# First layer of a graph network on one core: waits taken apart in a loop of two interleaved streams, long rows stored, edge weights and two-pass operations spread out

## The chip, the cores and the metric

The kernel runs on one core of one Trainium2 chip. The metric is the device time of one execution in microseconds; the figure for a kernel is the median of its timed runs. The engines go by the names of the profile: PE is TensorE (PEld its weight loads), DVE is VectorE, ACT is ScalarE, POOL is GpSimd, SP is SyncE. Each engine runs its own instructions in order and waits on semaphores for the others; a DMA is issued from one engine's queue (SP, ACT or POOL).

## The reference

A graph of 3125 nodes (256 features) and 100,000 edges, sorted by destination, goes through four blocks, each with a residual: a graph attention block, a mixture of experts of which two are shared by all tokens, a block of graph convolutions, and a mixture of experts routed by token. Only the first attention layer of the first block is touched here:

```python
h = (x @ W).reshape(N, H, C)                  # H = 4 heads of C = 256
al_s = jnp.einsum('nhc,hc->nh', h, a_src)
al_d = jnp.einsum('nhc,hc->nh', h, a_dst)
e = jax.nn.leaky_relu(al_s[src] + al_d[dst], NEG_SLOPE)
m = jax.ops.segment_max(e, dst, num_segments=N)
ex = jnp.exp(e - m[dst])
denom = jax.ops.segment_sum(ex, dst, num_segments=N)
alpha = ex / denom[dst]
out = jax.ops.segment_sum(h[src] * alpha[:, :, None], dst, num_segments=N)
```

The edges include one loop for each node. Here `x` is the layer-normed input and `W` is 256 by 1024.

## The kernel before

`FirstLayer.run` does the first attention layer. It sums normed input rows by edge and multiplies by `W` afterwards, so an edge costs a row of 256 numbers and four weights, not 1024 numbers. The edges come in 391 chunks (`C1`) of 256, sorted by destination. Three streams of work are interleaved by hand in one loop:

- **Counting** (`count_step`, all 391 chunks). It makes a matrix of how often each pair of nodes is joined, which later layers use. `make` builds two one-hot matrices for a chunk: `hot_key` on DVE (L1668), and `hot_lo` either on DVE (L1671) or, for two chunks in three after the first 20, on ACT in two passes, Abs (L1674) and Relu (L1677). `multiply` takes their product on PE (L1685). The product's columns go into the accumulator `acc` at a place that is read from a register: `keep` copies all columns but the first on ACT (L1702), and `add` adds the first column on DVE (L1707), because the first column may already hold counts of the chunk before. In round i the chunk i is made, i - 1 multiplied, i - 3 added and i - 2 kept.
- **Edges** (`edge_step`, chunks from 108 on, 283 of them, in batches of four). `fetch` gathers table rows of the sources on POOL (L1794, two gathers a chunk) into a ring of 12 chunks; a gather is issued once PE has used the slot's old rows. `window` fetches the destination terms of a batch and the places of its edges (L1804, L1807, on SP's queue). `pick_terms` (PE, L1831) lays a term beside each edge; `weigh_edges` adds source terms (DVE, L1840), takes the two slopes' maximum (DVE, L1843) and the exponent (ACT, L1844); `spread_edges` (DVE, L1850) puts the weights into the matrix that `multiply_edges` (PE, L1864) multiplies by the rows; `add_edges` adds the result into `agg` (DVE, L1877). `place_edges` (L1815, L1818) prepares the places of the batch after the next.
- **Dense** (`dense_step`, 100 steps). The first 256 destinations have so many edges that their weights are made for all sources: `exponent` on ACT in two passes, slope (L2031) and exponent (L2033), `weigh` on DVE (L2038), and the product on PE (L2047).

A round of the loop is a count step, one small task (clearing a piece, or the product by `W`, L1990 with its copy L2001), as many edge steps as are due, and any dense steps that are due. `in_order` then fixes the order of PE, DVE and ACT as it was traced, so each engine's queue is the program's order; SP and POOL follow the scheduler. PSUM banks: three for counts, two for the edges' sums (`ps_edge`, a chunk takes bank c % 2), two for the dense sums (`ps_po1`), one for everything else (`ps_aux1`).

Ahead of the loop, under its own fixed order of DVE: the bounds of the chunks (`bounds`), the layer norm in five groups (`norm_rows`), `attention_vectors` (L1574: products of `W` by the attention rows, 16 for this layer and 16 for the next), `keys`, `edge_starts`, `check`, then PE transposes of the normed rows (L2147) and the products of them by the attention vectors (L2157). `first_terms` turns these into source terms (stored in 32-byte pieces beside the table's rows, L1602), destination terms (`terms`, L1606) and the loops' weights (`loops`, L1615); the last two are stored in pieces of 16 bytes, one for each node. `new_sums` starts each piece of `agg` from the loops (L1920 loads the weights, L1930 multiplies).

## Time and profile before

| | |
|---|---|
| median of 3 runs | 2530.73 us (2528.81 to 2531.22) |
| the profiled execution, its own time | 2545.83 us |
| its span, first to last instruction | 2544.0 us |
| mean granted TensorE clock | 0.91 |
| first layer, up to its last store | 0 to about 1072 us |
| its loop | about 105 to 1042 us |
| busy in the whole span | PE 2125.6, DVE 1361.0, ACT 1138.6, POOL 819.5 us |

A row of the profile names a line, an engine, an operation and its tiles; behind the bar stand its busy time and its mean duration, and behind the second bar the time for which the engine was idle just before it, with what ended that idle time. Line numbers are those of the kernel before; in the changed kernel the same operations stand 14 to 63 lines lower.

### The profile page before, as it was taken

The page shows a single profiled execution, that of the slowest core. Times are in us where ns is not written, and L with a number is a line of the kernel's source. Part 1 is how long each engine was busy: PE and PEld are TensorE (multiplying, and loading weights), DVE is VectorE, ACT ScalarE, POOL GpSimd, SP SyncE. Part 2 cuts the span into 40 slices and gives each one's busy share as a digit, 9 for nine tenths or more (in the row PEclk, how much of TensorE's full clock was granted, in tenths as well). Part 3 has the DMA queues.
Part 4 walks back from the last instruction along what each step waited for, and adds up shares of the span by engine and source line. Part 5 has one row for each costly group of instructions (what it writes and reads, how often), then busy time and mean ns, then how long its engine had stood idle before and what let it go on. Part 6 is the DMA issues. An engine that isn't in the chain of part 4 may idle for free. (4 is left out here: it accounts for less than half of the span.)

```text
span 2544.0 us, 36033 instructions
## 1 busy us (share of the span) xinstructions
PE 2125.6 (84%) x10501; PEld 1746.2 (69%) x10501; DVE 1361.0 (53%) x4372; ACT 1138.6 (45%) x2504; POOL 819.5 (32%) x803
## 2 busy tenths in 40 slices
PE   4377668777878778698999979998999897999996
PEld 3255556665656556487888858876887676888885
DVE  8767557556677667514888844343334665122221
ACT  3277545555555555352444425443434443222321
POOL 2655566656566766020000030000000313222221
PEclk8578888888998988899999989998999998899998
DMA  7633446464556656599222110003424436667773
GB/s 246 118 95 90 132 120 173 112 180 126 165 152 191 184 142 180 172 384 300 93 76 67 51 50 1 1 1 129 127 67 156 164 110 208 170 180 209 233 209 74
DMA packets 247282, 358.52 MB, mean 141 GB/s; under 512 B 47768, under 2 KB 188371, under 8 KB 243362
## 3 DMA queue, kind: packets, MB, share of 16 engines
q1 hardware_dynamic: 203906, 256.29, 31.9%
q0 software_dynamic: 39600, 95.33, 14.6%
q10 hardware_dynamic: 3568, 4.47, 0.7%
q8 instruction: 89, 1.46, 0.2%
q14 instruction: 119, 0.97, 0.1%
HBM read 270.26 MB, written 86.20 MB: 140 GB/s over the span
## 5 line engine op out<-in xcount | busy, mean ns | idle before, releaser
L1794 POOL DMA_INDIRECT edge_rows<-table,pick x566 | 594.1, 1050 | 329.2 <-issue 116.4
L1864 PE MATMUL edge_sums<-edge_moves,edge_rows 128*128 128x120 f32 x2264 | 362.3, 311 | 66.4 <-issue 33.8
L1864 PEld LDWEIGHTS edge_sums<-edge_moves,edge_rows 128*128 128x128 f32 x2264 | 335.8, 222 | 113.3 <-issue 50.3
L1092 PE MATMUL po<-parts,cnt_r 128*128 128x512 f32 x1250 | 318.3, 410 | 16.7 <-ACT cnt_r L1086 9.5
L1685 PE MATMUL ps<-hot_key,hot_lo 128*128 128x350 f16 (+2 forms) x782 | 210.4, 360 | 125.7 <-ACT hot_lo L1677 51.5
L1702 ACT CAST acc<-ps 128x325 f32 (+2 forms) x391 | 178.4, 456 | 262.4 <-DVE acc L1707 109.1
L1092 PEld LDWEIGHTS po<-parts,cnt_r 128*128 128x128 f32 x1250 | 240.1, 195 | 70.4 <-ACT cnt_r L1086 10.3
L854 PE MATMUL po<-h,w 128*128 128x257 f32 x1250 | 278.1, 383 | 7.2 <-DVE w L845 4.9
L854 PEld LDWEIGHTS po<-h,w 128*128 128x128 f32 x1250 | 236.8, 191 | 44.0 <-DVE w L845 6.9
L1668 DVE TENSOR_SCALAR hot_key<-iota_key,key 128x350 f16<-128x350 f16 (+2 forms) x782 | 233.0, 327 | 7.1 <-PE ps L1685 3.7
L2625 ACT ACTIVATE hid<-ph,ffn_b 128x256 f32<-128x256 f32 (+1 forms) x232 | 105.8, 456 | 263.5 <-PE ph L2623 257.9
L1685 PEld LDWEIGHTS <-hot_lo 128*128 128x128 f16 x782 | 76.0, 109 | 183.8 <-ACT hot_lo L1677 68.6
L2623 PE MATMUL ph<-xe,ffn_w 128*128 128x256 f32 (+1 forms) x928 | 194.4, 367 | 3.6 <-DMA ffn_w<-in_L_ffn_W 3.6
L2633 PE MATMUL py<-ffn_w,hid 128*128 128x256 f32 x848 | 189.8, 381 | 1.4 <-ACT hid L2625 1.4
L2638 POOL DMA_INDIRECT out<-y,to x53 | 82.6, 1559 | 316.8 <-DVE y L2637 162.4
L2623 PEld LDWEIGHTS ph<-xe,ffn_w 128*128 128x128 f32 x928 | 165.1, 194 | 26.9 <-DVE rt_xt L1023 4.0
L2633 PEld LDWEIGHTS py<-ffn_w,hid 128*128 128x128 f32 x848 | 159.3, 191 | 22.2 <-ACT hid L2625 1.8
L839 ACT ACTIVATE z<-z,att_cols 128x640 f32<-128x640 f32 x125 | 103.1, 828 | 153.5 <-DVE z L837 130.7
L1674 ACT ACTIVATE hot_lo<-iota_key,lo 128x128 f16<-128x128 f16 x494 | 169.0, 391 | 0.0
L1877 DVE TENSOR_TENSOR agg<-agg,edge_sums 128x126 f32 (+1 forms) x283 | 87.2, 308 | 133.0 <-PE ps L1685 35.3
L1086 ACT CAST cnt_r<-cnt_h 128x1920 fp32r<-128x1920 f16 x50 | 89.9, 1799 | 116.3 <-PE po L1092 106.0
L2299 POOL IOTA earlier<- 128x128 f32 x1 | 0.2, 243 | 395.7 <-PE po L1092 395.7
(410 smaller groups left out, 3295.1 us busy)
## 6 DMA issues: line engine op xcount, KB each, us to landing
ffn_w<-in_L_ffn_W SPq DMA_DIRECT2D x58, 1024.0 KB
cnt_h<-cnt SPq DMA_DIRECT2D x50, 800.0 KB
rows<-blank SPq DMA_DIRECT2D x109, 258.0 KB
cnt<-acc SPq DMA_DIRECT2D x50, 400.0 KB
cnt<-cnt SPq DMA_DIRECT2D x25, 800.0 KB
normed<-first_out SPq DMA_DIRECT2D x20, 640.0 KB
first_out<-first SPq DMA_DIRECT2D x56, 192.0 KB
edge_turn<-places SPq DMA_DIRECT2D x283, 32.0 KB
```

Of the source, the lines that this page charges most:

```text
L839: nc.scalar.activation(z, z, AF.Exp, bias=cols[:, 0, j:j + 1], scale=-1.0)
L854: nc.tensor.matmul(pos[i][:, :D + 1], lhsT=w[:, ts(i, P)], rhs=moving[:, j, :D + 1], start=(j == 0), stop=(j == NB - 1))
L1092: nc.tensor.matmul(pos[b], lhsT=c[:, j - j0, ts(b, P)], rhs=parts[i][:, j].rearrange("p a m -> p (a m)"), start=(j == 0), stop=(j == NB - 1))
L1668: nc.vector.tensor_scalar(h[:, u, :NB * w], self.wide[:, :NB * w], self.key[:, t:t + 1], None, op0=ALU.is_equal)
L1674: nc.scalar.activation(l[:, u, :], self.wide[:, :P], AF.Abs, bias=self.lo[:, t:t + 1], scale=-1.0)
L1685: self.nc.tensor.matmul(ps[:, :n], lhsT=l[:, u, :], rhs=h[:, u, :n], start=(u == 0), stop=(u == CT - 1))
L1702: self.nc.scalar.copy(self.acc[g][:, :, ds(o + 1, width(c) - 1)], self.parts[c][:, :, 1:])
L1794: self.nc.gpsimd.indirect_dma_start(out=self.ring[:, e % (RB * BT), :], out_offset=None, in_=self.table, in_offset=bass.IndirectOffsetOnAx ...
L1864: nc.tensor.matmul(ps[:, f * 4 * w:f * 4 * w + EW], lhsT=self.rows_of(m)[:, e, ts(f, P)], rhs=self.spread[m % 3][:, e * 5 * w:e * 5 * w + EW],
L2623: nc.tensor.matmul(ph, lhsT=w1[:, c, ts(f, P)], rhs=xe[:, c, :], start=(c == 0), stop=(c == 1))
L2625: nc.scalar.activation(hid[:, f, :], ph, AF.Gelu, bias=b1[:, f:f + 1])
L2633: nc.tensor.matmul(py, lhsT=hid[:, f, ts(i, P)], rhs=w2[:, f, :], start=(f == 0), stop=(f == NF - 1))
```

## The change

It has these parts, all in the first layer:

- `keep` and `add` are declared free of each other in one direction: the copy of a chunk no longer waits for additions of earlier chunks.
- The Relu of `hot_lo` moves into `sharpen`, behind `multiply`, `add` and `keep` of the round; the slope of a dense step is taken behind `make`, its exponent behind `sharpen`.
- The weights of a batch of edges: sum at the start of step 1, slopes' maximum at the end of step 1, exponent in step 2, spreading in step 3 of the batch before; it was sum, maximum and exponent at the end of step 0, spreading in step 2.
- The edges' sums go round four half banks; the dense sums have one bank and the rest two.
- The places of a batch come with one DMA instead of four. Registers are loaded four chunks ahead of their first use.
- At most one dense step is done in a round.
- Ahead of the loop: the attention vectors come before the norm, the rows are transposed and multiplied group by group right behind their norm, and the subtraction of the last row of `W` goes from POOL to DVE. The terms and the loops' weights are transposed on PE and stored as long rows.

```diff
     def where(self, name, c, row, n, engines, top):
 
         regs = self.regs
-        if (name, c) not in regs:
-            c8 = c // RG * RG
+        for c8 in (c // RG * RG, (c + RG // 2) // RG * RG):
+            if (name, c8) in regs or c8 >= n:
+                continue
             _, v = self.nc.values_load_multi_w_load_instructions(
...
+    def turn_rows(self, g, u1, pl, pool, turn):
+
+        nc, k = self.nc, self.k
+        xt = pool.tile([P, 2, GW], F32, name="xt", bufs=2)
+        for i in range(GB):
+            b, at = g * GB + i, ts(i, P)
+            pt = turn.tile([P, 512], F32, name="turn")
+            for c in range(2):
+                nc.tensor.transpose(pt[:, ts(c, P)], k.x[:, b, ts(c, P)], k.ident)
+            nc.scalar.copy(xt[:, :, at], pt[:, :2 * P].rearrange("p (c n) -> p c n", c=2))
+            for c in range(2):
+                nc.tensor.matmul(pl[:, 8 * b:8 * b + 8], lhsT=xt[:, c, at], rhs=u1[:, c, :],
+                                 start=(c == 0), stop=(c == 1))
+        nc.sync.dma_start(self.turned[:, :, g * GW:(g + 1) * GW], xt)
...
-        nc.sync.dma_start(self.terms.rearrange("o (b p k) -> (o p) b k", p=P, k=n), t)
+        pt = turn.tile([P, 512], F32, name="turn")
+        for i in range(n):
+            nc.tensor.transpose(pt[:NB, ts(i, P)], t[:, :, i], k.ident)
+        flat = tmp.tile([NB, P, n], F32, name="terms_flat")
+        nc.scalar.copy(flat, pt[:NB, :].rearrange("b (k p) -> b p k", k=n))
+        nc.sync.dma_start(self.terms.rearrange("o (b f) -> (o b) f", b=NB),
+                          flat.rearrange("b p k -> b (p k)"))
...
-        nc.sync.dma_start(self.loops.rearrange("(b p) k -> p b k", p=P), own)
+        pt = turn.tile([P, 512], F32, name="turn")
+        rows = (NB - DB) * n
+        nc.tensor.transpose(pt[:rows, :P], own.rearrange("p b k -> p (b k)"), k.ident)
+        flat = tmp.tile([rows, P], F32, name="loops_flat")
+        nc.scalar.copy(flat, pt[:rows, :P])
+        nc.sync.dma_start(self.loops.rearrange("b (k p) -> (b k) p", k=n), flat)
...
+        self.hots[c] = h, l
+
+    def sharpen(self, c):
         if not (c < EARLY or c % 3 == 0):
-            nc.scalar.activation(l, l, AF.Relu, bias=1.0, scale=-1.0)
-        self.hots[c] = h, l
+            l = self.hots[c][1]
+            self.nc.scalar.activation(l, l, AF.Relu, bias=1.0, scale=-1.0)
...
-        self.nc.scalar.copy(self.acc[g][:, :, ds(o + 1, width(c) - 1)], self.parts[c][:, :, 1:])
+        ins = self.nc.scalar.copy(self.acc[g][:, :, ds(o + 1, width(c) - 1)],
+                                  self.parts[c][:, :, 1:])
+        self.tc.declare_no_dep(ins.ins, group=f"first_columns{g}",
+                               reason="a copy's columns lie behind all earlier chunks' first ones")
...
-        self.nc.vector.tensor_tensor(col, col, self.parts.pop(c)[:, :, 0:1], ALU.add)
+        ins = self.nc.vector.tensor_tensor(col, col, self.parts.pop(c)[:, :, 0:1], ALU.add)
+        self.tc.add_to_no_dep_group(f"first_columns{g}", ins.ins)
...
-    def count_step(self, i):
+    def count_step(self, i, beside=(lambda: None,) * 2):
         if i < C1:
             self.make(i)
+        beside[0]()
         if 1 <= i <= C1:
             self.multiply(i - 1)
         if 3 <= i <= C1 + 2:
             self.add(i - 3)
         if 2 <= i <= C1 + 1:
             self.keep(i - 2)
+        if i < C1:
+            self.sharpen(i)
+        beside[1]()
...
-        self.ps_out = ctx.enter_context(tc.tile_pool(name="ps_po1", bufs=2, space=PSUM, reuse_waits="tile"))
-        self.aux = ctx.enter_context(tc.tile_pool(name="ps_aux1", bufs=1, space=PSUM, reuse_waits="tile"))
+        self.ps_out = ctx.enter_context(tc.tile_pool(name="ps_po1", bufs=1, space=PSUM, reuse_waits="tile"))
+        self.aux = ctx.enter_context(tc.tile_pool(name="ps_aux1", bufs=2, space=PSUM, reuse_waits="tile"))
...
-        self.ps_edge = [psum.tile([P, 512], F32, name=f"edge_sums{i}") for i in range(2)]
-        for ps in self.ps_edge:
-            nc.vector.memset(ps[:, :4 * CW + EW], 0.0)
+        banks = [psum.tile([P, 512], F32, name=f"edge_sums{i}") for i in range(2)]
+        for ps in banks:
+            nc.vector.memset(ps, 0.0)
+        self.ps_edge = [banks[i % 2][:, i // 2 * 256:(i // 2 + 1) * 256] for i in range(4)]
...
         if c == 0:
-            self.turn_e[m] = self.work.tile([P, CE], F32, name="edge_turn", bufs=3)
+            t, n = self.work.tile([P, CE], F32, name="edge_turn", bufs=3), self.size[m]
+            at = self.places[C0 + m * BC:C0 + m * BC + n, :]
+            self.nc.sync.dma_start(t[:n * s, :], at[:, None, :].to_broadcast([n, s, CE]))
+            self.turn_e[m] = t
...
-        at = self.places[C0 + m * BC + c:C0 + m * BC + c + 1, :]
-        self.nc.sync.dma_start(self.turn_e[m][c * s:(c + 1) * s, :], at.to_broadcast([s, CE]))
...
+        if m + 1 < NBAT and q == 1:
+            self.sum_terms(m + 1)
         if m + 1 < NBAT and q == 2:
+            self.weigh_edges(m + 1)
+        if m + 1 < NBAT and q == 3:
             self.spread_edges(m + 1)
...
-        if m + 1 < NBAT and q == 0:
-            self.weigh_edges(m + 1)
+        if m + 1 < NBAT and q == 1:
+            self.pick_slope(m + 1)
```

In `run`, cut to its order:

```diff
-                nc.gpsimd.tensor_tensor(w1, w1, last_row[:, None, :].to_broadcast([P, 2, 4 * D]),
-                                        ALU.subtract)
...
                 u1 = tmp.tile([P, 2, 8], F32, name="u1")
+                self.attention_vectors("1", tmp, u1, w1.rearrange("p c (k f) -> p k c f", k=4))
...
                     if g > 0:
                         next(groups[g - 1])
-                self.count_starts(tmp)
-                self.attention_vectors("1", tmp, u1, w1.rearrange("p c (k f) -> p k c f", k=4))
+                        self.turn_rows(g - 1, u1, pl, tmp, turn)
...
+                parts = self.first_terms(sd, pool, tmp, turn)
+                next(parts)
+                self.count_step(i)
+                next(parts)
+                for i in range(i + 1, i + 6):
+                    self.count_step(i)
...
-                while s < len(self.steps) and i > d0 + 3 and \
-                        s * (C1 - 12 - d0) <= (i - d0 - 3) * len(self.steps):
+                if due:
                     self.dense_step(s)
                     s += 1
```

## The prediction

> **What bounds the kernel now.** I read the windows by stage first, then, for the stage of the change alone, the waits and the groups by line. Columns of the first: stretch (us), its length, busy us of each engine (instructions), granted TensorE clock, DMA share, GB/s.
>
> ```profile
> 41.00:105.00 64.00, 29.94 (x163) 25.02 (x161) 49.23 (x196) 10.59 (x30) 23.47 (x25) 0.56 0.67 139
> 105.00:276.00 171.00, 117.36 (x685) 90.05 (x685) 122.97 (x566) 118.23 (x373) 99.79 (x97) 0.77 0.40 110
> 276.00:1042.00 766.00, 594.09 (x3280) 463.13 (x3280) 496.50 (x1734) 421.86 (x1090) 488.75 (x477) 0.88 0.54 152
> ```
>
> All edits lie in the first layer, 0 to 1072 us. Its loop has two parts: A, 105 to 276, counts with 0.37 edge chunks in each round; B, 276 to 1042, with 0.94 chunks and 0.4 dense steps (the first L2031 stands at 276.5). In neither is one engine full: PE is busy in 594 of B's 766 us, DVE in 497, ACT in 422. So the rounds are held by hand-overs. The waits of B, longest first (engine, line, waited for: total us, times, longest):
>
> ```profile
> POOL edge_rows L1794 <- PE edge_sums L1864: 71.4, 60, 4.5
> ACT acc L1702 <- DVE acc L1707: 51.1, 42, 7.0
> ACT edge_p L1844 <- DVE edge_p L1843: 50.6, 30, 5.5
> PE ps L1685 <- ACT hot_lo L1677: 34.7, 17, 4.8
> PE edge_sums L1864 <- DVE agg L1877: 30.2, 21, 4.3
> DVE edge_p L1840 <- PE aux L1831: 27.8, 10, 5.1
> DVE edge_p L1840 <- DMA edge_rows<-table,pick: 19.1, 9, 4.9
> PE aux L1831 <- ACT first L2001: 9.6, 7, 4.5
> ```
>
> Read from PE: it waits for ACT's hot_lo, ACT is late because its copy (L1702) waited for DVE's one-column addition (L1707), or because its exponent (L1844) stood in order behind a DVE that itself waited for PE's L1831 in the same edge step. That is a ring PE, DVE, ACT, PE. What PE lost is in the groups of B (busy, mean ns | idle before it, releasers):
>
> ```profile
> L1864 PE MATMUL edge_sums<-edge_moves,edge_rows 128*128 128x120 f32 x1896 | 295.7, 306 | 66.2 <-issue 33.6 <-DVE agg L1877 30.2 <-DVE acc L1660 1.2
> L1685 PE MATMUL ps<-hot_key,hot_lo 128*128 128x500 f16 (+1 forms) x506 | 150.0, 381 | 64.2 <-ACT hot_lo L1677 34.7 <-DVE acc L1707 13.1 <-issue 9.2
> L1990 PE MATMUL aux<-agg,w_all 128*128 128x384 f32 x192 | 74.7, 513 | 11.7 <-ACT first L2001 8.3 <-issue 3.3
> L1831 PE MATMUL aux<-window,edge_turn 128*128 128x16 f32 (+1 forms) x232 | 34.9, 265 | 22.1 <-ACT first L2001 9.6 <-DVE edge_turn L1818 4.0 <-issue 3.8
> L1794 POOL DMA_INDIRECT edge_rows<-table,pick x452 | 474.1, 1049 | 249.4 <-issue 95.9 <-PE edge_sums L1864 71.4 <-PE ps L1685 28.9
> ```
>
> The 66, 64, 12 and 22 us, with 5.4 before L2068 and 2 of the rest, are PE's 172 idle us of B. The last line sets a floor: successive gathers stand 0.30 us apart even when nothing holds them (943 ns + 0.30 = 1.25 us in quiet stretches), so 452 x (1.049 + 0.30) = 610, and 25 loads of x_rows x (0.59 + 0.30) = 22: POOL needs 632 us of B's 766.
>
> **The change, part by part.**
>
> 1. ACT's copy no longer waits for the addition (keep, add declared apart). In the changed program's order the copy waits for PE and ACT alone; the addition still waits for the copy, rightly. The edge weights' sum, maximum, exponent and spread go to q = 1, end of 1, 2 and 3 instead of three at q = 0: each has a round between it and the engine that feeds it. Instructions are the same in number. PE's share: 34.7 (hot_lo) + 13.1 (L1707 late) = 48. ACT's own waits (51.1 at L1702; 50.6 and, behind L1840, 33.4 at L1844) are not added to it: they are the same time seen from ACT.
>
> 2. DVE stops standing at L1840 for PE, so its addition L1877 is earlier. PE waits 30.2 for it and 33.6 for what the trace does not name. I take half of the 30.2, 15, and none of the 33.6. The bounds are 0 and 64; the half, because DVE also waits for PE at L1877 (35.3 + 34.6 us), a hand-over that stays.
>
> 3. Four half banks for edge_sums instead of two banks. Row first: PE waits 30.2 us for L1877, and four independent buffers would take the 15 left, and perhaps the 33.6. The Trainium skill, PSUM — Partial Sum Buffer, section "PSUM bank collisions raise a hardware error", says that TensorE's write and VectorE's read may not meet in one bank even at different addresses, and that waits must go by bank. By that rule chunk c still waits for the addition of c - 2, as before; the changed program's order has exactly that wait. No run so far has two engines in one bank, so the trace does not test the rule itself. I take 0. By the row alone the sum would be 15 to 49 us better.
>
> 4. Banks: aux 1 to 2, po 2 to 1. The waits of PE for L2001 (9.6 + 8.3) and some for L2063 go: 19. Against it, at three changes of head PE's next po waits for two DVE pairs and two L2063 (0.47 us each), about 2 us in queue: -6.
>
> 5. window: one DMA of places per batch, not four (283 down to 71). Each issue is about 0.36 us on SP's queue, whose waits end no chain in B: 0; if the batch's rows come late, L1818 waits (DVE edge_turn, 4.0 us now). Registers loaded four chunks earlier: the 49 + 36 loads of 0.6 us on DVE (by their source line) stay the same in number, and none is named as a wait: 0.
>
> 6. Slope (L2031) and exponent (L2033) of the dense part, and Abs and Relu of hot_lo, get other operations between them. In the timeline two Abs in a row of 391 ns take 0.69 us, so they overlap by 0.09; Relu, which needs its Abs, starts 0.03 after it. Estimate 0.12 us a pair: in B (168 + 100) x 0.12 = 32 us of an ACT that is 55% busy: 0 there. In A (79 pairs, ACT 118 of 171 busy) up to 9.
>
> B: 48 + 15 + 19 - 6 = 76, so 690 us, against POOL's 632: POOL would be 92% occupied, with the ring's five chunks of slack, so the floor is near but does not bind yet.
>
> A: ACT waits 17.9 us for L1707 (same list for 105 to 276) and PE 16.8 for hot_lo. One of them, plus item 6, bounds 0 to 27; I take 17.
>
> **Start.** SP's queue shows the long way of short pieces: terms is issued at 73.1, its first reader at 84.7; loops at 78.4, its reader at 90.3; and DVE then stands:
>
> ```profile
> 94.47 3.94 DVE L1930 TENSOR_TENSOR agg<-loop_x,by_node 128x1024 f32<-128x1024 f32 x2 [13.34 <-DMA by_node<-loops]
> ```
>
> In the change 25 rows of 2 KB replace terms' 3,200 pieces of 16 bytes, and 92 rows of 512 bytes replace loops' 2,944. The price is 5 transposes (0.28), two copies (0.5), before the store. Against it, DVE's order is now worse ahead of them. attention_vectors (16 x 0.345 = 5.5 us) stands before norm_rows, and needs both att rows: POOL's queue had moved 1,536 KB when w_last landed at 16.3, and ACT's must move 1,808 KB up to the second of them, so an estimate at the same rate is 19. With half of the products behind the second row, a matmul and a subtraction, the norms start near 22.9 instead of 18.0; turn_rows puts 5 copies (1.65) and 10 + 10 matmuls in each group, some 4.8 us for a group on ACT, so the last group ends near 48 (34 before). Then keys 7.5, starts 3.7, L2112's subtraction now on DVE (twice L1982's 1.22 = 2.4), counts 1.4, check 4.9: sd is copied at about 68 instead of 63.8. One count step instead of six before s_terms gives 4 back, so the table is stored at about 73, as before. terms then reaches its readers about 6 us earlier and loops 10: by_node is there near 84 instead of 94.5. I take 10 (bounds: -4, if nothing but the order counts, to 14).
>
> Sum: 76 + 17 + 10 = 103 us. The profiled execution took 2545.83 us (span 2544.0): 2443. The median of the runs shown is 15.1 lower: 2428.
>
> **Rivals.**
> - Everything elastic goes: B falls to POOL's floor plus 8 (640), A by 25, the start by 14: -165, 2366. For: PE's granted clock is 0.88 in B and 0.77 in A, 1.00 in later, fuller stretches, so less idling may also shorten its matmuls. Against: 4.9 us waits of DVE for rows show that POOL is already late at times.
> - The waits move. Rows (19.1), the two-bank hand-over (64) and "issue" take what hot_lo leaves: half of item 1 and none of 2: B -37 (24 + 19 - 6), A -8, start 0: -45, 2486. For: in order engines with one round of slack; the start's DVE order is really longer.
> - Slower: the spread (L1850) now stands one edge step, not two, ahead of its multiply at q = 0. If ACT comes to the exponent a step late, DVE stands at the spread, and behind it the one-hot keys, additions and so PE. An edge step is 766 / 238 = 3.2 us; 59 batches x 3.2 = 190 - 103 = +87, 2615. It decides from 1.7 us a batch. Against: ACT is 55% busy and loses its longest wait.
> - The apart declaration does nothing because ACT waits for PE at L1702 anyway (11.9 + 21.9 us now): then item 1 is half, the second case.
>
> **How the numbers follow.** Likeliest 0.58 (2400 to 2460 itself); floor 0.14; waits move 0.22; spread late 0.06. From the floor's middle to beyond the second rival: 2380 to 2495. A measurement of this kernel tells about 0.2% (5 us) from no change. Faster 0.93, same 0.02 (the tail of the second rival), slower 0.05.
>
> **What would show it.** Right: ACT acc L1702 <- DVE acc and ACT edge_p <- DVE edge_p gone or under 15 us; the last L1685 near 940 instead of 1041.6; PE's idle in B under 100; PE edge_sums <- DVE agg still there; terms' readers near 80 and the first L1864 near 95 instead of 104.9; sd's copy later than 63.8. Wrong: idle before the spread or its multiply of 1.7 us a batch; waits for edge_rows' DMA over 50 us; POOL at 1.25 us a gather throughout (the floor); a start longer than 105.

## The result, and the profile after

The changed kernel takes 2511.93 us (median of 4 runs, 2508.54 to 2515.16), beside 2530.97 us of the kernel before on the same chip (2528.81 to 2535.8): a ratio of 0.9929, with an interval of 0.9905 to 0.9952. It is faster by 0.7%, 19 us where 103 were forecast, and lies outside the range. The profiled execution took 2515.16 us (span 2513.4), 30.7 us less than the profiled one before.

The experiments ran in groups, each beside its own runs of the kernel before; these took 2529 to 2545 us in some groups and 2428 to 2431 us in others, so medians are compared inside a group; stages are also set beside those of another group, of the same kind unless the text says otherwise.

The spans split by the events that the prediction used: the first multiply of edges (L1864, now L1913), the first slope of the dense part (L2031, now L2082), the last multiply of counts (L1685, now L1716).

| stage | before | after | change | forecast |
|---|---|---|---|---|
| start, to the first multiply of edges | 104.9 | 121.0 | +16.1 | -10 |
| A | 171.6 | 157.7 | -13.9 | -17 |
| B | 765.3 | 734.4 | -30.9 | -76 |
| the rest | 1502.2 | 1500.3 | -1.9 | 0 |

The windows of the changed kernel by stage: stretch, length, busy us of PE, PEld, DVE, ACT and POOL (instructions), granted TensorE clock, DMA share, GB/s.

```profile
41.00:121.00 80.00, 27.66 (x123) 21.97 (x124) 52.53 (x206) 17.10 (x43) 26.62 (x30) 1.00 0.45 135
121.00:279.00 158.00, 106.31 (x678) 83.75 (x679) 113.86 (x556) 105.66 (x370) 91.34 (x89) 0.84 0.38 107
279.00:1013.00 734.00, 579.47 (x3288) 455.93 (x3288) 479.82 (x1740) 383.01 (x1093) 487.91 (x479) 0.90 0.55 159
```

In B, DVE lost 17 us of work and ACT 39, but PE is still idle for 155 of 734 us (172 of 766 before; under 100 was the sign of a right forecast). The waits of B in the changed kernel (waited for: total us, times, longest) show that this idle time has changed its names:

```profile
ACT acc L1733 <- PE ps L1716: 74.2, 39, 5.5
ACT acc L1733 <- remote: 52.2, 18, 5.0
DVE agg L1926 <- remote: 50.7, 21, 4.2
...
PE edge_sums L1913 <- issue: 34.8, 23, 4.3
PE edge_sums L1913 <- DVE agg L1926: 33.2, 23, 4.9
...
PE ps L1716 <- ACT hot_lo L1709: 20.4, 13, 4.0
```

The same two engines in the kernel before:

```profile
DVE agg L1877 <- remote: 29.0, 10, 6.1
...
ACT acc L1702 <- remote: 14.2, 5, 6.0
```

The copy's wait for the addition (51.1 us before) is gone, and the exponent's wait for DVE fell from 50.6 to 9.4. In their place the copy waits for PE, and the copy and DVE's addition L1926 wait longer for "remote" (103 us together, 43 before): there a semaphore was updated, but no instruction that updates it had ended shortly before. The groups of B (busy, mean ns | idle before, releasers):

```profile
L1834 POOL DMA_INDIRECT edge_rows<-table,pick x454 | 473.7, 1043 | 224.2 <-issue 98.9 <-PE edge_sums L1913 38.7 <-PE ps L1716 35.8
L1913 PE MATMUL edge_sums<-edge_moves,edge_rows 128*128 128x120 f32 x1903 | 289.3, 300 | 75.8 <-issue 34.8 <-DVE agg L1926 33.2 <-DVE edge_p L1881 6.7
L1716 PE MATMUL ps<-hot_key,hot_lo 128*128 128x500 f16 (+1 forms) x507 | 148.1, 377 | 48.3 <-ACT hot_lo L1709 20.4 <-remote 7.9 <-DVE acc L1741 7.1
L2042 PE MATMUL aux<-agg,w_all 128*128 128x384 f32 x192 | 73.6, 507 | 1.1 <-DVE edge_p L1881 0.6 <-issue 0.5
L1982 DVE TENSOR_TENSOR agg<-loop_x,by_node 128x1024 f32<-128x1024 f32 x17 | 20.7, 1215 | 7.6 <-issue 4.2 <-DMA loop_x<-x_turned 3.4
```

The first row gives POOL's queue 454 x (1.043 + 0.30) = 610 us, 632 with the loads, as before, of 734. The second row's idle time is longer than before (75.8 against 66.2), while that before the counts' multiply fell from 64.2 to 48.3 and that before L2042 from 11.7 to 1.1. A row whose idle time grows under "issue" while the named waits go is where the search starts. The timeline of the changed kernel in the middle of B (start, duration, engine, line; in brackets the idle time just before):

```profile
608.69 0.59 PE L1716 MATMUL ps<-hot_key,hot_lo 128*128 128x500 f16 x2
...
609.93 0.94 POOL L1834 DMA_INDIRECT edge_rows<-table,pick  x1 [0.30 <-PE ps L1716]
...
612.19 0.34 DVE L1926 TENSOR_TENSOR agg<-agg,edge_sums 128x180 f32 x1 [2.23 <-remote]
612.29 0.46 ACT L1733 CAST acc<-ps 128x325 f32 x1 [3.26 <-remote]
612.38 0.94 POOL L1834 DMA_INDIRECT edge_rows<-table,pick  x1 [1.51 <-remote]
...
612.59 1.15 PE L1913 MATMUL edge_sums<-edge_moves,edge_rows 128*128 128x120 f32 x8 [3.31 <-issue]
```

From 609.96 to 612.19 PE, DVE and ACT all stand, and POOL joins them at 610.87. PE had ended at 609.28; what DVE and ACT wait for is its work. The trace also records when each semaphore is updated, the signal by which an engine tells the others that a piece of work is done. Of PE's semaphore one update is on record at 609.74, the next at 612.12, and five more follow up to 612.37. So PE's work had been done for 2.8 us when they came, and DVE, ACT and POOL start as they come.

Late updates are common in B. Of PE's updates there, 284 of the 703 on record come more than 0.5 us after the last PE instruction that makes one (271 of 676 before); idle time that ended with such an update adds up to 162 us of ACT and 118 of DVE (63 and 107 before). The 0.5 us is only a line for counting; in B of `e11_weights_back`, a run further down, PE's updates come 13 ns after their instruction (median) and none later than 15. Some 150 of PE's updates, and half of DVE's, have no record in B of the changed kernel.

Stretches like this one, over 0.3 us with PE, DVE and ACT all idle, add up to 61 us of B in the changed kernel and 51 before (summed from the records of the traces).

### The profile page after: what moved, and what is told of

It reads as the page before. It is cut to its first block, busy times and chain, and to the rows that moved or that the text cites. A ratio compares the mean times of both kernels' runs of the same rounds, so it can differ in the third digit from the quotient of the medians.

```text
span 2513.4 us, 35928 instructions
## 1 busy us (share of the span) xinstructions
PE 2105.1 (84%) x10508; PEld 1737.6 (69%) x10508; DVE 1335.5 (53%) x4374; ACT 1088.0 (43%) x2506; POOL 809.0 (32%) x802
## 5 line engine op out<-in xcount | busy, mean ns | idle before, releaser
L1834 POOL DMA_INDIRECT edge_rows<-table,pick x566 | 587.9, 1039 | 306.8 <-issue 125.5
L1913 PE MATMUL edge_sums<-edge_moves,edge_rows 128*128 128x120 f32 x2264 | 349.9, 304 | 89.3 <-issue 48.3
L1913 PEld LDWEIGHTS edge_sums<-edge_moves,edge_rows 128*128 128x128 f32 x2264 | 325.5, 216 | 133.6 <-issue 62.5
L1716 PE MATMUL ps<-hot_key,hot_lo 128*128 128x350 f16 (+2 forms) x782 | 205.7, 355 | 133.7 <-ACT hot_lo L1709 39.3
L1716 PEld LDWEIGHTS <-hot_lo 128*128 128x128 f16 x782 | 72.2, 107 | 189.9 <-ACT hot_lo L1709 64.8
L1926 DVE TENSOR_TENSOR agg<-agg,edge_sums 128x126 f32 (+1 forms) x283 | 87.0, 308 | 175.7 <-remote 50.7
```

The costliest lines, as they stand in the source:

```text
L1716: self.nc.tensor.matmul(ps[:, :n], lhsT=l[:, u, :], rhs=h[:, u, :n], start=(u == 0), stop=(u == CT - 1))
L1834: self.nc.gpsimd.indirect_dma_start(out=self.ring[:, e % (RB * BT), :], out_offset=None, in_=self.table, in_offset=bass.IndirectOffsetOnAx ...
L1913: nc.tensor.matmul(ps[:, f * 4 * w:f * 4 * w + EW], lhsT=self.rows_of(m)[:, e, ts(f, P)], rhs=self.spread[m % 3][:, e * 5 * w:e * 5 * w + EW],
```

## The experiments

Each edit is made in the changed kernel unless it says "before". Times in us; the stages come from each run's profile.

| run | median | kernel before, same group | first multiply of edges | A | B |
|---|---|---|---|---|---|
| e1_vectors_back | 2513.65 | 2532.06 | 116.7 | 160.6 | 734.9 |
| e2_gathers_held | 2508.20 | 2532.06 | 100.7 | 172.5 | 733.8 |
| e3_half_product | 9799.83 | 2532.06 | 119.7 | 149.2 | 730.5 |
| e4_half_gathers | 2339.23 | 2532.06 | 118.9 | 129.7 | 569.8 |
| e5_short_gathers | 2533.18 | 2528.76 | 121.1 | 160.8 | 746.0 |
| e6_half_from_sp | 2345.97 | 2528.76 | 120.8 | 129.7 | 597.1 |
| e7_half_filled | 2431.22 | 2528.76 | 120.2 | 178.9 | 636.5 |
| e8_half_added | 2453.18 | 2528.76 | 121.1 | 163.5 | 672.9 |
| e9_before_half_gathers | 2399.41 | 2430.69 | 103.2 | 163.6 | 611.7 |
| e10_gathers_aside | 2610.61 | 2430.69 | 102.7 | 215.9 | 760.9 |
| e11_weights_back | 2380.04 | 2430.69 | 100.7 | 140.0 | 636.7 |
| e12_copy_waits | 2394.15 | 2430.69 | 104.9 | 148.7 | 636.9 |
| e13_changed_again | 2522.55 | 2544.79 | 121.3 | 159.7 | 739.1 |
| e14_before_half_again | 2413.37 | 2544.79 | 107.4 | 163.8 | 619.5 |
| e15_half_again | 2336.33 | 2544.79 | 120.0 | 127.8 | 569.2 |
| e16_held_and_rows_from_sp | 2516.18 | 2544.79 | 101.0 | 179.9 | 742.6 |
| e17_half_weights_back | 2327.46 | 2428.17 | 100.3 | 136.7 | 571.1 |
| e18_half_copy_waits | 2348.84 | 2428.17 | 104.6 | 148.8 | 576.7 |

### The start: the order of DVE, or the gathers

The first gather stands at 85.5 (77.8 before), the first multiply at 121.0. `e1_vectors_back` puts the next layer's attention vectors back ahead of the copy of sd.

```diff
                 self.check(tmp)
+                self.attention_vectors("2", tmp, u2, ...)
                 sd = tmp.tile([P, NB, 8], F32, name="sd")
...
-                self.attention_vectors("2", tmp, u2, ...)
                 k.in_order({}, start, [mybir.EngineType.DVE])
```

> The changed kernel with attention_vectors of the next layer (16 products on DVE) back ahead of the copy of sd, as in the kernel before. Theory 'order': the pools of the loop can only open after these products, so the first gather comes at about 78 instead of 85.5 us, the first L1913 at about 110 to 113 instead of 121.0, and the median falls by 8 to 10 us (2502 to 2504). Rival 'gathers against DVE': the 24 gathers in a row keep DVE standing wherever they lie; moved 7 us earlier they meet other DVE work, the 16 us of unnamed waiting on DVE stays, and the first L1913 stays above 115: 0 to -5 us.

Ratio 0.9925 (0.9903 to 0.9947), the same as the change. The first gather stays at 85.3 and the multiply comes at 116.7, where 110 to 113 were expected of the order: DVE's order there accounts for about 4 of the 16 us at most. `e2_gathers_held` issues only the first batch's 8 gathers at once; the other 16 of the ring wait for the first spread.

```diff
-            for c in range(RB * BC):
+            for c in range(BC):
                 self.fetch(c)
...
-            self.spread_edges(0)
+            spread = self.spread_edges(0)
+            for c in range(BC, RB * BC):
+                for ins in self.fetch(c):
+                    tc.add_manual_dep(ins.ins, spread.ins.name, SYNC)
```

> The changed kernel with only the first batch's 8 gathers let go ahead; the other 16 of the first ring wait for the spread of the first batch's weights (L1899). Theory 'gathers against DVE': the slope of the first batch, which stood 7.6 us before DVE took it, and the other unnamed waits of DVE between 96 and 118 us, about 16 us together, come from gathers being issued back to back; with POOL silent they fall under 3 us and the first L1913 stands near 106 instead of 121.0; the median falls by 8 to 15 us. Rival 'something else' (rows landing, windows' loads, instruction loading): the wait stays, the first L1913 stays at 118 to 121, and the later batches' rows come later: 0 to +10 us.

The first multiply comes at 100.7, 20 us earlier, with nothing else moved ahead of it. A grows by 15, which takes most of it back: 2508.20 us, ratio 0.9898 (0.9862 to 0.9934), which does not tell it from the change. So in this group the 16 gathers are what makes the start late. The timeline of DVE in the changed kernel shows where:

```profile
108.70 0.19 DVE L1881 TENSOR_TENSOR edge_p<-aux,edge_rows 128x32 f32<-128x32 f32 x1 [1.11 <-PE aux L1872]
110.10 0.26 DVE L1699 TENSOR_SCALAR hot_lo<-iota_key,lo 128x128 f16<-128x128 f16 x1 [1.21 <-issue]
117.95 0.19 DVE L1888 SCALAR_TENSOR_TENSOR edge_p<-edge_p,edge_rows 128x32 f32<-128x32 f32 x1 [7.59 <-issue]
```

L1888 waits, by the program, only for DVE's own L1881, and starts 9.06 us after it ended. DVE's semaphore tells the same: L1881 and L1699 update it and end at 108.89 and 110.36, and no update of it is on record between 106.38 and 115.13. With the 16 gathers held, no update of DVE's between the first gather and the first multiply is later than 0.2 us. In `e11_weights_back` (a group of the other kind; the start is not edited) the second starts 0.04 us after the first has ended, with the same 24 gathers:

```profile
99.28 0.12 DVE L1881 TENSOR_TENSOR edge_p<-aux,edge_rows 128x32 f32<-128x32 f32 x1
99.44 0.19 DVE L1888 SCALAR_TENSOR_TENSOR edge_p<-edge_p,edge_rows 128x32 f32<-128x32 f32 x1
```

### The loop: PE, or the gathers

`e3_half_product` leaves out one of the two halves of each edge product, so half of the sums is missing; only its loop is read, because what follows works on other values (8799 us behind the loop, instead of 1500). `e4_half_gathers` leaves out the second of the two gathers of a chunk behind the first ring; the slot keeps the rows of an earlier chunk.

```diff
-        for f in range(2):
+        for f in range(1, 2):
```

```diff
-        for e in range(c * CT, (c + 1) * CT):
+        for e in range(c * CT, (c + 1) * CT if c < RB * BC else c * CT + 1):
```

> The changed kernel with the first half of every edge product left out (f = 0: two of the four multiplies a chunk; the sums of the first 128 columns of a row stay unmade). It takes away about half of L1913's 290 busy us from PE in the dense part B (279 to 1013 us). Theory 'PE is the bound of B': B falls from 734 by 100 to 145 us. Rival 'hand-overs between engines bound B': DVE's and ACT's work and every wait stay in place, B falls by less than 50. Between: PE's work and hand-overs take turns, 50 to 100.

> The changed kernel with one of the two gathers of every chunk behind the first ring left out (the ring keeps older rows there). POOL's 480 issues in B become about 240. Theory 'PE and hand-overs': POOL has slack, B stays at 734 within 10 us. Rival 'POOL is near enough to the floor to bind' or 'gathers keep DVE standing in B too': B falls by 20 to 60 us.

The window of B with half the product:

```profile
269.00:999.00 730.00, 510.89 (x2336) 368.50 (x2334) 476.91 (x1740) 382.16 (x1094) 483.50 (x478) 0.82 0.57 160
```

PE does 69 us less (half of 290 was taken out, but the granted clock fell from 0.90 to 0.82), and B is 4 us shorter: PE is not the bound. With half the gathers B falls by 164 us, to 569.8, where at most 60 were expected, and the late updates all but vanish: 21 of PE's, where 284 were. The next four runs ask what it is about a gather, all behind the first ring. `e5_short_gathers` keeps their number and halves their bytes (rows of 128 numbers from another array); the other three replace the second gather of a chunk: `e6_half_from_sp` by a plain load of the same bytes on SP's queue, `e7_half_filled` by two fills on POOL (349 and 606 ns), `e8_half_added` by an addition on POOL (829 ns). The rows that enter the products are then not the edges' rows.

```diff
+            if c >= RB * BC:
+                slot, rows = slot[:, :P], self.turned.rearrange("p c (b f) -> (p c b) f", f=P)
...
+            if c >= RB * BC and e % CT:
+                self.nc.sync.dma_start(slot, self.table[:P, :])
+                continue
...
+                self.nc.gpsimd.memset(slot, 0.5)
+                self.nc.gpsimd.memset(self.idle_a, 0.5)
...
+                self.nc.gpsimd.tensor_add(slot[:, :D], self.idle_a, self.idle_b)
```

> The changed kernel with as many gathers as before, but behind the first ring each brings rows of 128 numbers (from another table) instead of 264: the other columns of the ring keep older rows. Same count of issues on POOL, less than half of the bytes. Theory 'issue' (POOL's 1.25 us for a gather is what the loop runs at): B (279 to 1013 us) stays at 734 within 15 us. Rival 'bytes' (the gathers' transfers or their landing): B falls towards the 570 us of the kernel with half of the gathers, by 80 us or more.

> The changed kernel with one of the two gathers of every chunk behind the first ring taken from POOL and replaced by a plain transfer of 128 whole rows from SP's queue into the same slot, under the same wait: the same bytes, half of POOL's issues (the rows are not those asked for). Theory 'issue': B near 570 to 600 us, as with half of the gathers left out. Rival 'bytes': B stays near 734.

> The changed kernel with one of the two gathers of every chunk behind the first ring replaced on POOL by two fills (the slot, and 600 numbers a partition beside it; about 0.9 us together), under the same wait: POOL is as long busy, writes SBUF, reads none and issues no transfer. Theory 'POOL is simply full' (its queue's time, whatever it does): B returns to about 700 to 734. Rival 'the gather itself' (its descriptors, or what it holds against DVE and PE): B stays at 570 to 600 us.

> The changed kernel with one of the two gathers of every chunk behind the first ring replaced on POOL by an addition of two tiles of 256 numbers into the slot (a like addition took 0.74 to 0.95 us elsewhere in the trace), under the same wait: POOL is about as long busy and reads SBUF as DVE does. Theory 'POOL is simply full': B returns to about 700 to 734, as with the fills. Rival 'POOL's reading holds DVE': B is longer here than with the fills by 30 us or more. Rival 'the gather itself': 570 to 600 us.

Half the bytes free nothing (B 746.0, 315 late updates of PE), and the same bytes by another queue free 137 us of the 164 (19 late). It is the number of gathers issued, not what they carry. Fills and additions that occupy POOL for about as long cost 67 and 103 us over `e4_half_gathers`, less than the theory that POOL is simply full had it (a B of 700 or more). They cost it in another way, with 19 late updates and none: they lengthen DVE, which is busy 470 us of B's 569 with half the gathers, 528 of 636 with fills and 624 of 672 with additions. The groups of B with half the gathers and nothing in their place, then with fills, then with additions:

```profile
L1696 DVE TENSOR_SCALAR hot_key<-iota_key,key 128x500 f16<-128x500 f16 (+1 forms) x506 | 157.9, 341 | 0.0
L2093 DVE TENSOR_TENSOR w<-z,cnt 128x256 f32<-128x256 f32 x100 | 42.0, 421 | 0.4 <-ACT z L2088 0.4
```

```profile
L1696 DVE TENSOR_SCALAR hot_key<-iota_key,key 128x500 f16<-128x500 f16 (+1 forms) x510 | 202.7, 425 | 0.0
L2099 DVE TENSOR_TENSOR w<-z,cnt 128x256 f32<-128x256 f32 x100 | 42.2, 423 | 0.0
```

```profile
L1696 DVE TENSOR_SCALAR hot_key<-iota_key,key 128x500 f16<-128x500 f16 (+1 forms) x506 | 224.3, 470 | 0.1
L2101 DVE TENSOR_TENSOR w<-z,cnt 128x256 f32<-128x256 f32 x100 | 58.0, 580 | 0.0
```

The one-hot keys, 341 ns, take 425 and 470; the product of two operands, 421 ns, stays at 423 beside fills, which only write, and takes 580 beside additions, which read. The Trainium skill, SBUF — State Buffer, section "Who interferes with whom", says just this: DVE and GpSimd share one pair of ports, scalar operations (tensor_scalar) can hold it, and an operation with two SBUF inputs meets only a GpSimd operation that reads. The gathers do not do it: hot_key takes 343 ns in the changed kernel with all of them. So this explains the cost of the replacements, and not that of the gathers.

`e10_gathers_aside` sends half of the gathers to two tiles that nobody reads, to keep their number and drop what waits for them.

```diff
+            if c >= RB * BC and e % CT:
+                slot = self.aside[c % 2]
```

> The changed kernel with one of the two gathers of every chunk behind the first ring sent to a tile beside the ring which nothing reads (the ring keeps older rows): as many gathers and bytes as in the changed kernel, but nobody waits for half of them and they wait for no slot of the ring, only for the last but one gather of their own. Theory 'waiting for rows and slots' (ring too short, POOL late): B near 570 to 610, as with half of the gathers. Rival 'a gather holds the others up wherever its rows go': B near 700 to 734.

It says nothing: the two tiles made waits of their own (POOL for their DMA, 37.8 us in 45 places), and DVE waited 178.6 us for the rows of the others. Two were too few. Nor could it have shown a gather holding others up: it fell in a group of 2430.69, where no update of PE, DVE or ACT comes late in B at all.

### With the gathers thinned, before and after

`e9_before_half_gathers` and `e14_before_half_again` make the edit of `e4_half_gathers` in the kernel before; `e15_half_again` is `e4_half_gathers` once more, and `e13_changed_again` the changed kernel, so that one group holds the kernel before and after, each with all and with half of the gathers.

> The kernel before with one of the two gathers of every chunk behind the first ring left out, as in e4 for the changed kernel (whose dense part B took 570 us so, 734 with all gathers). Theory 'the gathers cover the hand-overs': the terms of the prediction for B (76 us) are there, but gathers set the pace of both kernels; without half of them B of the kernel before (765) falls to 640 to 670 only, 70 to 100 above the changed kernel's 570. Rival 'the terms were too large in themselves': B falls to 590 to 610, about 32 above 570, as it is with all gathers.

> The changed kernel once more, as the anchor of this group: the kernel before took about 2430 us in the group of e9 to e12 and 2530 in the two groups before it, so runs are only compared inside one group. If this group is of the 2530 kind: 2505 to 2515 us, B 734. If of the 2430 kind: theory 'POOL's issue of gathers is the floor': B at 632 to 645, as in e11 and e12 which each lack one part of the change, and 2370 to 2385 us.

> As e9 (the kernel before with one of two gathers of a chunk left out behind the first ring), now in one group with e13 and e15. Theory 'the terms for B are real and hidden by the gathers': its B is 40 to 80 us longer than that of e15, while with all gathers the changed kernel's B is only 25 to 32 us shorter than before's. Rival 'the terms were too large in themselves': 15 to 35 us longer.

> As e4 (the changed kernel with one of two gathers of a chunk left out behind the first ring), now in one group with e13 and e14: B at 560 to 580 us, in either kind of group, because no gather is waited for.

The windows of A and B, thinned, of the kernel before and then of the changed one:

```profile
107.00:271.00 164.00, 111.94 (x687) 85.08 (x686) 122.04 (x568) 117.76 (x374) 53.99 (x53) 0.82 0.28 80
271.00:891.00 620.00, 541.16 (x3280) 430.81 (x3280) 488.91 (x1733) 418.73 (x1090) 261.94 (x251) 0.94 0.48 139
```

```profile
120.00:248.00 128.00, 91.81 (x677) 72.95 (x678) 109.65 (x556) 103.55 (x370) 47.71 (x45) 0.95 0.30 85
248.00:817.00 569.00, 514.45 (x3289) 422.63 (x3289) 470.15 (x1740) 381.34 (x1093) 257.16 (x252) 0.97 0.51 152
```

Thinned, the change brings 77 us (2413.37 to 2336.33): start +13, A -36, B -50, the rest -3 (it works on other values and takes 1517 to 1521 us in both). With all gathers in the same group it brings 22 (2544.79 to 2522.55; ratio 0.9909, 0.9873 to 0.9945). Put the other way, all the gathers cost the kernel before 131 us and the changed one 186: 55 us of what the change frees are lost to them again. Thinned, the three-engine stretches of B all but vanish (2 us before the change, 6 after).

The groups say the same. The kernel before took 2430.69 us in one and 2544.79 in another, 114 apart; thinned (`e9_before_half_gathers`, `e14_before_half_again`) 2399.41 and 2413.37, 14 apart. What differs between the groups is for the most part what the gathers cost. (`e9_before_half_gathers` has a B of 611.7, between its two forecasts.) The records of semaphores show where it lies. PE's updates in B:

| run | kernel before, same group | gathers | made | on record | over 0.5 us late |
|---|---|---|---|---|---|
| changed kernel | 2530.97 | all | 855 | 703 | 284 |
| e13_changed_again | 2544.79 | all | 855 | 703 | 315 |
| e15_half_again | 2544.79 | half | 852 | 687 | 30 |
| e14_before_half_again | 2544.79 | half | 834 | 659 | 19 |
| e9_before_half_gathers | 2430.69 | half | 834 | 831 | 0 |
| e11_weights_back | 2430.69 | all | 844 | 829 | 0 |
| e12_copy_waits | 2430.69 | all | 855 | 821 | 0 |

So late updates in number take both: all the gathers, and a group of the longer kind.

### Single parts

`e11_weights_back` takes the edge weights' steps back to where they were; `e12_copy_waits` takes the free copy back (the declaration is left out).

```diff
-        if m + 1 < NBAT and q == 1:
-            self.sum_terms(m + 1)
         if m + 1 < NBAT and q == 2:
-            self.weigh_edges(m + 1)
-        if m + 1 < NBAT and q == 3:
             self.spread_edges(m + 1)
...
-        if m + 1 < NBAT and q == 1:
+        if m + 1 < NBAT and q == 0:
+            self.sum_terms(m + 1)
             self.pick_slope(m + 1)
+            self.weigh_edges(m + 1)
```

> The changed kernel with the steps of the edges' weights as in the kernel before (sum, maximum and exponent at the end of step 0, spreading in step 2). The prediction's step 1 put about half of 48 us on these steps: then B is 20 to 45 us longer (median 2530 to 2555). Theory 'the gathers set the pace': the waits move to other places, B within 12 us of 734 (median 2505 to 2525).

> The changed kernel without the declaration that keep and add are free of each other, so that ACT's copy L1733 waits for DVE's addition of the chunk before again. The prediction's step 1 put about half of 48 us in B on it, and up to 17 in A: the median is 25 to 50 us longer (2537 to 2562). Theory 'the gathers set the pace': within 15 us in B, up to 15 in A (2512 to 2540).

Both fell in a group where the kernel before takes 2430.69: ratios 0.9784 (0.9761 to 0.9806) and 0.9847 (0.9825 to 0.9869). B is 636.7 and 636.9, whichever part is taken back, where all forecasts had it at 719 or more. The window of B and the first waits of `e11_weights_back`:

```profile
241.00:877.00 636.00, 536.80 (x3286) 437.46 (x3284) 477.86 (x1739) 380.09 (x1092) 485.15 (x478) 0.93 0.65 184
```

```profile
ACT edge_p L1893 <- DVE edge_p L1888: 146.9, 53, 7.6
DVE edge_p L1881 <- DMA edge_rows<-table,pick: 67.9, 24, 5.9
...
POOL edge_rows L1834 <- issue: 57.0, 187, 0.3
```

This is the floor of the prediction's first rival: POOL's pauses in B are 0.3 us, all but one, the rows come late, and the exponent stands for 147 us in front of a floor that nothing there can shorten. Two different kernels end within 0.2 us of each other and 5 us above the 632 that the prediction worked out for POOL's queue.

`e16_held_and_rows_from_sp` adds to `e2_gathers_held` the 25 loads of x_rows from SP's queue instead of POOL's, 22 us off that floor.

```diff
-                nc.gpsimd.dma_start(self.x[:, b, :], x_in[ts(b, P), :])
+                nc.sync.dma_start(self.x[:, b, :], x_in[ts(b, P), :])
```

> The changed kernel with the first ring's last 16 gathers held until the first batch's weights are spread (e2), and the 25 loads of x_rows that stand between POOL's gathers issued from SP's queue instead. Theory 'POOL's issue of gathers is the floor': POOL's time in B falls by 25 x (0.60 + 0.30) = 22 us, so B by about 20 in a group of the 2430 kind, by 0 to 20 in one of the 2530 kind; with e2's 5 us the median is 5 to 25 us under e13's. Rival: SP's queue stands at these loads behind PE's dense products and brings the windows late: longer than e13.

Ratio 0.989 (0.9858 to 0.9922) beside 0.9909 of the change: not told apart. POOL is 467 us busy in B instead of 483 in `e13_changed_again`, and B is not shorter (742.6 beside 739.1). In this group POOL's queue is not what B stands at.

`e17_half_weights_back` and `e18_half_copy_waits` are `e11_weights_back` and `e12_copy_waits` with thinned gathers.

> The changed kernel with half of the gathers behind the first ring left out (as e15: start to the first L1913 120 us, A 128, B 569) and the steps of the edges' weights as in the kernel before. The prediction's step 1 (48 us in B for this and the free copy together, up to 17 in A for the copy) gives this part about half: B 590 to 605, A 128 to 135. Rival 'the other edits (banks, two-pass operations, shorter multiplies) made the 50 us in B and 36 in A': B within 8 us of 569.

> The same base as e17, with ACT's copy L1733 waiting for DVE's addition again, as in the kernel before. Step 1 gives the free copy about half of 48 us in B and most of A's gain: B 585 to 600, A 140 to 160. Rival 'the other edits made the gain': B within 8 us of 569, A within 8 of 128.

They fell in a group of 2428.17, so `e15_half_again` is of the other kind: beside it B is longer by 2 without the weights' steps and by 7.5 without the free copy, A by 9 and 21. The neighbour of their own kind is `e9_before_half_gathers` (B 611.7, A 163.6), and beside it B is still 41 and 35 us shorter, A 27 and 15. Neither part alone carries the 50 us of B, as the rival had it; both taken back at once wasn't run.

## Why the prediction missed the size

**The failed step is "So the rounds are held by hand-overs", and with it item 1's 48 us in B (hot_lo 34.7, L1707 13.1).** It took PE's named waits for the price of the program's order, which another order would take away. In the groups of 2530 to 2545 us the engines wait in large part for updates that come late while gathers are in flight, under both orders. ACT's wait for the addition went as forecast, but PE's own two waits only fell, 34.7 to 20.4 and 13.1 to 7.1: 20 of the 48. The late updates stayed (271 and 284 of PE's) and the waiting moved on to them. Thinning the gathers frees 164 us, and then the same change brings 50 of its 76 in B instead of 31. The list of waits that the step was read from shows no row that ends in "remote"; there are four over 14 us in B (29.0, 27.7, 14.9 and 14.2).

The gathers stood in the sum only as a floor: "POOL would be 92% occupied, so the floor is near but does not bind yet". By the letter that was right here (632 of 734 us), and in a group of 2430 us two kernels had B on the floor itself. But in the groups of 2530 to 2545 us the gathers act before POOL's queue is full: they hold the changed kernel's B at 730 to 746 whatever is done to PE, to the bytes or to POOL's other loads.

**The second rival** named this: "The waits move". Its 37 for B is near the measured 31, but by luck, since its reason ("engines in order with one round of slack") was not the one found. Thinned, B gives 50, and the single parts do not show that these are item 1's.

**Item 2 (15) and item 3 (0).** PE's wait for DVE's addition was 30.2 and is 33.2: item 2 brought nothing, and the two-bank hand-over stays, as item 3 had it. **Item 4 (19 - 6)**: the waits before L2042 are gone (11.7 to 1.1), those before L1872 stay (22.1 to 21.2).

**Item 6, credited 0 in B.** ACT is busy 383 us in B instead of 422, near the 32 us worked out. "An ACT that is 55% busy" was the reason to give it nothing. Another part was not foreseen: the multiply in `new_sums` takes 1.215 us instead of 1.999 (the row of L1930 shown before: two in 3.94), 17 times, 13 us of DVE, now that the loops' weights lie as rows and are no longer read by node at a stride. With the 50 us of B unassigned, the two are candidates; no run takes them back alone.

**A, -17, measured -14; thinned, -36.** The size was met by luck, as a balance of two errors: thinned, the parts are worth twice that (the free copy up to 21, `e18_half_copy_waits` across groups), and the gathers take the rest.

**The start, -10, measured +16.** The details stood: sd copied at 68.3 (forecast "about 68"), the loops' multiply at 88.4 instead of 94.5 (forecast 84). The step that failed here is that by_node is what the first multiply of edges waits for. That multiply hangs on the edge weights' chain, which was late with all gathers in flight (9 us between two DVE instructions); the 24 gathers go out from 85 to about 115 (24 x 1.25), over just this chain. Held back it stands at 101, 4 us better than before. In groups of 2430 us it stands at 100 to 105, where the kernel before has 103 (`e9_before_half_gathers`). The forecast of 95 was not reached there either.

**The slower rival** (the spread late, 1.7 us a batch) did not come: 11 us of idle time before the spread in all. (Its 87 us make 2618, not 2615.) **The clock** rose as the first rival had it: 0.88 to 0.90 in B, and 0.97 thinned, where the edge multiply takes 282 ns instead of 300.

**What stays open.** The records show that updates come late, not what holds them: a load of instructions, for one, stands in the 3 us before such an update no more often (25% of 122 places in B) than before any moment (27%). Nor is it shown why one group has it and another not, since the same chip gave both, or whether the recording of the runs has a part in it. The changed kernel itself was not run in a group of 2430 us, so whether `e11_weights_back` is better than it isn't known. No run that leaves nothing out beat the change inside a group by more than the intervals.

## What to carry to other kernels

Before hand-over waits are added up to a gain, thin the feeder that runs beside them (half the gathers) and see whether the waits are there without it: a run that takes the suspect away says more than a list of who waited for whom. Where all engines stand at once and the release is "remote" or "issue", look for the moment at which the semaphore was updated before taking the ring of waits for the cause: here, taking named waits out of the ring in good part renamed the time. Count the indirect gathers by number, 1.25 us of queue each here and in some groups more in what they hold up, not by bytes.

## What the runs showed of the hardware

- With gathers in flight, updates of semaphores between engines that have nothing to do with them can come late: 9.06 us instead of 0.04 between two dependent DVE instructions, and 2.2 us with PE, DVE and ACT all idle inside the loop. 284 of 703 updates of PE came over 0.5 us late, 21 with half of the gathers, none in groups of 2430 us. Half the bytes freed nothing, half the number 164 us.
- POOL's own data operations lengthen DVE's: the one-hot keys from 341 to 425 ns beside fills and 470 beside additions, a product of two operands only beside additions (580 instead of 421). The issue of gathers does not (343 ns for the keys).
- A DVE multiply of 128x1024 with one operand read at a stride took 1.999 us, with rows 1.215.
- The same kernel took 2430 us in one group of runs and 2545 in another; thinned of half its gathers it took 2399 and 2413.
